# A two-layer convolution/attention hybrid on one core: the first image's tokens in the second image's bands, the last bands' linear layers between the attention's products

## The chip, the core and the metric

The kernel runs on one core of a Trainium2 chip. A core has a matrix engine (TensorE, here PE, with its weight loads PEld), a vector engine (VectorE, DVE), a scalar engine (ScalarE, ACT), a general engine (GpSimd, POOL) and a queue that issues DMA transfers (SyncE, SP; ACT issues some too). The engines run side by side, each works through its own instructions in order, and semaphores make one wait for another. Matrix products are written to PSUM, which has eight banks of 128 partitions by 512 floats.

The metric is device time in microseconds of one execution. Everything is computed in float32.

## What is computed

The input is two images of 128 channels on a grid of 64 by 64. Layer 0 works on positions of the grid, layer 1 on the same 4096 positions as a sequence of tokens. Cut to what matters (`_ln` is a layer norm over channels, `_na2d` an attention of four heads in which each position sees the 7 by 7 window around it):

```python
# layer 0
v = group_norm(x, G=32)                      # per image
r = v
y = _ln(v);  y = _na2d(y, qkv_w, qkv_b, rpb, proj_w, proj_b)
y = _ln(y);  y = y @ w1.T + bl1
v = y + r;   r = v
y = _ln(v);  y = relu(y @ w2.T + bl2)
y = _ln(y);  y = y @ w3.T + bl3
x = x + (y + r)
# layer 1, t = tokens of x
t = t + attention(_ln_t(t))                  # 4096 x 4096 with the diagonal masked,
t = t + spectral_ffn(_ln_t(t))               # long convolutions, four branches
```

The attention of layer 1 uses its normalised tokens as queries, keys and values alike. (In the reference's text the function for it is written for any length; here the length is 4096.)

## The kernel before

**Layer 0** goes through 16 bands: image 0 then image 1, eight bands of eight grid rows each. A band's work is cut into named pieces, and `PLAN` gives every piece a time. Band number k is shifted by k times `PERIOD`; all pieces of all bands are sorted by that time, and inside `tc.manual_schedule` the instructions of PE, DVE, ACT and POOL are issued in exactly this order. The numbers set only the order: nothing waits for a time. DMA issues on SP are not part of the manual order.

A band's pieces are

- `p.*`, the input: `p.xg` (group norm applied, POOL, line 445), `p.tok` (four transposes to tokens), layer norm (`p.bn` statistics, `p.pw` the power on POOL, `p.zd`/`p.za` the scaling on DVE and ACT, `p.tr` transposes back, `p.zT` copy), then `p.q`, `p.k`, `p.v` with their copies. `p.vc` also stores v to DRAM in eight transfers and loads the windows (`vw`, 98 positions each) in up to sixteen.
- `u0.*` to `u3.*`, the attention in four units of 128 positions: `S` the scores (line 515, sixteen small products in four banks), `t0` to `t3` adding the bias table with a minimum (DVE, line 528), `e0` to `e3` the exponentials (ACT, line 538), `T0`, `T1` turning them (PE, line 551), `c0`, `c1` copies (ACT and DVE), `V` the product with v (line 573).
- `r.*`, the division by the sums, ending in `r.att` (line 604), and `t.*`, the tail: projection, layer norm 1, `w1`, residual `t.x2`, layer norm 2, `w2`, relu, layer norm 3, `w3`, and `t.fin`, which writes the band back to `xa` (line 660). `t.add` on POOL adds the original x into `x2` (line 636).

The p-pieces of a band lie up to 2.4 periods ahead of its first unit, the tail ends 4.2 periods after it. The PSUM banks are dealt in rings: `ps_m` of five (`bank()`), `ps_t` of two (`tokens`), `ps_o` of one for the unit products.

**Between the layers** `tokens(0, bank)` makes layer 1's tokens of image 0: eight groups of four tiles, each with transposes of `xa` (line 190), an add on DVE that also brings in the constant row `b3row` (line 193), statistics (lines 151, 152, 161), scaling to `tok` (DVE, line 169), transposes (line 180) and a copy to `cm` (ACT, line 204). Its 32 steps are events after the last band's start, mixed with the last bands' tails.

**Layer 1** runs `attention(0, fill)`: blocks of products from `cm` (line 743), exponentials on ACT (line 750), turning (line 757), and products with `tok` (lines 771, 796). After every block `fill()` takes one step of waiting work: first what follows a finished chunk (`urgent`), then a list, `[filters(), tokens(1, bank)]`. Then the same for image 1, and last the convolution (line 1104 on).

At the start SP loads image 0 in four transfers, ACT the weights; 32 small transfers, 16 on each of the two, bring the relative position table into `rev`, which is cleared on POOL beforehand (line 131) and turned by PE (`flipped`, line 246). All of it uses the space of `tok` and `cm` of image 0.

Of the kernel before, what the change touches and what calls it, by code (L numbers as in the profile page):

```python
# [48 lines left out]
    "p.xg": -6335, "p.tok": -6075, "p.bn": -5991, "p.pw": -5688, "p.zd": -5538, "p.nb": -5465, "p.za": -5233,  # L49
    "p.tr": -5130, "p.zT": -4875, "p.k": -4750, "p.kT": -4353, "p.q": -4242, "p.qT": -4132, "p.v": -3805,  # L50
    "p.vc": -3550, "u0.S": 0, "u0.t2": 105, "u0.t0": 150, "u0.e2": 165, "u0.t1": 195, "u0.e0": 230, "u0.t3": 240,
    "u0.e1": 295, "u0.e3": 360, "u0.T0": 440, "u0.T1": 495, "u0.c0": 510, "u0.c1": 565, "u1.S": 662, "u0.V": 752,
    "u1.t1": 768, "u1.t2": 812, "u1.e1": 828, "u1.t0": 857, "u1.t3": 902, "u1.e0": 917, "u1.e2": 1021,
    "u1.e3": 1086, "u1.T0": 1178, "u1.T1": 1233, "u1.c0": 1248, "u1.c1": 1303, "u2.S": 1325, "u1.V": 1415,
    "u2.t3": 1430, "u2.e3": 1490, "u2.t2": 1494, "u2.t0": 1539, "u2.e2": 1555, "u2.t1": 1584, "u2.e0": 1620,
    "u2.e1": 1685, "u2.T0": 1765, "u2.T1": 1820, "u2.c0": 1872, "u2.c1": 1890, "u3.S": 1988, "u2.V": 2079,
    "u3.t0": 2092, "u3.t1": 2137, "u3.e0": 2152, "u3.t2": 2182, "u3.e1": 2235, "u3.t3": 2250, "u3.e3": 2310,
    "u3.e2": 2375, "r.rden": 2390, "r.rb": 2422, "u3.T1": 2455, "u3.T0": 2510, "u3.c1": 2525, "r.rdT": 2565,
    "u3.c0": 2580, "r.c": 2658, "u3.V": 2740, "r.att": 2935, "t.proj": 3483, "t1.bn": 3722, "t1.pw": 3862,
    "t1.nb": 4022, "t1.za": 4053, "t1.zd": 4279, "t1.tr": 4580, "t1.zT": 4726, "t.w1": 4848, "t.x2": 4958,  # L60
    "t.tx": 5048, "t.add": 5197, "t2.bn": 5244, "t2.pw": 5476, "t2.zd": 5668, "t2.nb": 5741, "t2.za": 5966,
    "t2.tr": 6925, "t2.zT": 7109, "t.w2": 7593, "t.y": 7759, "t.ty": 8175, "t3.bn": 8584, "t3.pw": 8837,
    "t3.zd": 9148, "t3.nb": 9220, "t3.za": 9256, "t3.tr": 9630, "t3.zT": 9880, "t.w3": 10880, "t.fin": 11057,
}
PERIOD = 2650
# [17 lines left out]
def kernel(  # L83
# [40 lines left out]
    b3row = fp.tile([P, P], F32, name="b3row")  # L124

# [5 lines left out]
    nc.gpsimd.memset(cm[0][0 : QT * QT, 0 : HEADS * NTAB * NTAB], 0.0)  # L131
# [49 lines left out]

    def tokens(b, bank):

        for n0 in range(0, NT, 4):
            pt = bank()
            for j in range(4):
                ph, f = divmod(n0 + j, FB)
                par, h = divmod(ph, 2)
                t0 = h * TH + 2 * f + par
                nc.tensor.transpose(  # L190
                    pt[:, j * P : (j + 1) * P], xa[b][:, t0 : t0 + 2 * FB * (P - 1) + 1 : 2 * FB], ident
                )
            nc.vector.tensor_tensor(
                tt[b][:, n0 : n0 + 4, :], pt.rearrange("p (j c) -> p j c", c=P),
                b3row.unsqueeze(1).to_broadcast([P, 4, P]), ALU.add,
            )
            yield
            stats = ln_statistics(tt[b][:, n0 : n0 + 4, :])
            yield
            ln_apply(tok[b][:, n0 : n0 + 4, :], tt[b][:, n0 : n0 + 4, :], stats)  # L200
            yield
            pt = bank()
            transposed(pt, tok[b][:, n0 : n0 + 4, :])
            nc.scalar.copy(cm[b][:, n0 * P : (n0 + 4) * P], pt)
            yield


    with ExitStack() as l0:
        wp = l0.enter_context(tc.tile_pool(name="l0_w", bufs=1))
        big = l0.enter_context(tc.tile_pool(name="l0_big", bufs=1))  # L210
        bp = l0.enter_context(tc.tile_pool(name="l0_band", bufs=2))
        ps_m = l0.enter_context(tc.tile_pool(name="l0_ps_m", bufs=5, space=PSUM))
        ps_t = l0.enter_context(tc.tile_pool(name="l0_ps_t", bufs=2, space=PSUM))
        ps_o = l0.enter_context(tc.tile_pool(name="l0_ps_o", bufs=1, space=PSUM))
        vdram = l0.enter_context(tc.tile_pool(name="l0_dram", bufs=1, space=bass.MemoryType.DRAM))
# [12 lines left out]
        tab = wp.tile([P, 6, HEADS, KEYS], F32, name="tab")  # L228
        for h in range(HEADS):
            for r in range(QT):  # L230
                lo, hi = 6 - min(r, 6), min(NTAB, 21 - r)
                src = bass.AP(
                    rpb_pad.tensor, (h * RPR + lo - 6 + r) * RPW + 50, [[1, QT], [RPW, hi - lo], [1, NTAB]]
                )
                (nc.sync if h % 2 else nc.scalar).dma_start(out=rev[r * QT : (r + 1) * QT, h, lo:hi, :], in_=src)
        nc.sync.dma_start(out=mask, in_=nc.inline_tensor(_window_masks(), "window_masks").ap())
        for c in range(4):
            nc.sync.dma_start(out=xa[1][:, c * 1024 : (c + 1) * 1024], in_=xin[1, :, c * 1024 : (c + 1) * 1024])

        def bank():  # L240
            return ps_m.tile([P, 512], F32, tag="bank", name="bank")

        def flipped(h):
            pb = bank()
            for half in range(2):
                nc.tensor.matmul(
                    pb[half * 64 : (half + 1) * 64, 0 : NTAB * NTAB], lhsT=flip[0:64, 64:128],
                    rhs=rev[:, h].rearrange("p n m -> p (n m)"), start=True, stop=True,
                )
            nc.scalar.copy(base[:, h].rearrange("p n m -> p (n m)"), pb[:, 0 : NTAB * NTAB])  # L250
# [28 lines left out]
        for i, (lo, be, col, row) in enumerate((  # L279
# [3 lines left out]
            pb = bank()  # L283
# [13 lines left out]
        pb = bank()  # L297
# [8 lines left out]
        wide = bp.tile([P, P], F32, tag="wide", name="wide", bufs=1)  # L306
        nc.vector.tensor_copy(wide, cb[:, C_3 : C_3 + 1].to_broadcast([P, P]))
        pb = bank()
        nc.tensor.transpose(pb[:, 0:P], wide, ident)
        nc.vector.tensor_copy(b3row, pb[:, 0:P])  # L310
# [3 lines left out]
        sp = l0.enter_context(tc.tile_pool(name="l0_s", bufs=2))  # L314
        mp = l0.enter_context(tc.tile_pool(name="l0_m", bufs=3))
        ls = l0.enter_context(tc.tile_pool(name="l0_ln", bufs=6))
# [21 lines left out]
        def to_tokens(src, ring=ps_t, tag="tokens"):  # L338
            pt = ring.tile([P, 512], F32, tag=tag, name="pt")
            for j in range(4):  # L340
                nc.tensor.transpose(pt[:, j * P : (j + 1) * P], src[:, j * P : (j + 1) * P], ident)
            return pt

        def linear(lo, zT):
            pl = bank()
# [3 lines left out]
        def group_norm(b):  # L349
# [11 lines left out]
            pb = bank()  # L361
# [6 lines left out]
            pb = bank()  # L368
# [15 lines left out]
        def norm_pieces(stage, src):  # L384
# [46 lines left out]
            def _(t, b, g):  # L431
                t[stage + "pz"] = bank()
# [25 lines left out]
        def _(t, b, g):  # L458
            t["qT"] = bp.tile([P, BAND], F32, tag="qT", name="qT", bufs=3)
# [12 lines left out]
        def _(t, b, g):  # L472
            pv = t["pv"] = bank()
# [7 lines left out]
        def _(t, b, g):  # L481
            v = bp.tile([P, 4, P], F32, tag="v", name="v")
# [11 lines left out]
        def windows(b, g):  # L494

            for u in range(4):
                vw = bp.tile([HK, 2, 2, P], F32, tag="vw", name="vw", bufs=6)
# [7 lines left out]
        def unit_pieces(u):  # L505
# [3 lines left out]
            def _(t, b, g):  # L509
                t[name + "S"] = [bank() for _ in range(HEADS)]  # L510
# [35 lines left out]
            def half_pieces(ch):  # L546
                @piece(f"{name}T{ch}")
                def _(t, b, g):
                    pt = t[f"{name}T{ch}"] = bank()
# [38 lines left out]
        def _(t, b, g):  # L588
            t["rb"] = bp.tile([P, 4 * HEADS, DH], F32, tag="rb", name="rb", bufs=1)
# [3 lines left out]
        def _(t, b, g):  # L593
            t["pr"] = to_tokens(t["rb"].rearrange("p a d -> p (a d)"), ps_m, "bank")

        @piece("r.c")
        def _(t, b, g):
            t["rdT"] = bp.tile([P, BAND], F32, tag="rdT", name="rdT", bufs=1)
# [8 lines left out]
        def _(t, b, g):  # L607
            pt = t["pp"] = ps_t.tile([P, 512], F32, tag="tokens", name="pt")
# [25 lines left out]
        def _(t, b, g):  # L634
            for nat, til in ordered(xa[b][:, rows_of(g)], t["x2"]):
# [25 lines left out]

        for _ in group_norm(0):
            pass
# [7 lines left out]
        for k, (b, g) in enumerate(order):  # L671
            t = {}
            for name, at in PLAN.items():
                events.append((at + k * PERIOD, lambda f=pieces[name], t=t, b=b, g=g: f(t, b, g)))
        for i in range(8):
            events.append((-1800 + 200 * i, lambda ci=4 + i // 4, h=i % 4: table(ci, h, nc.gpsimd)))
            events.append((2 * PERIOD + 600 * i, lambda ci=2 + i // 4, h=i % 4: table(ci, h, nc.gpsimd)))

        gn1, tok0 = group_norm(1), tokens(0, bank)
        for i in range(7):  # L680
            events.append((2 * PERIOD + i * PERIOD // 3 + 50, lambda: next(gn1)))
        for i in range(NT):
            events.append((len(order) * PERIOD + i * PERIOD // 11, lambda: next(tok0)))
        events.sort(key=lambda e: e[0])
        engines = mybir.EngineType
        with tc.manual_schedule(engines={engines.PE, engines.DVE, engines.Activation, engines.Pool}):
            for _, f in events:
# [12 lines left out]
    with ap_:  # L700
# [19 lines left out]
        tt[1] = tp.tile([P, NT, P], F32, name="tt1")  # L720
        tok[1] = tp.tile([P, NT, P], F32, name="tok1")
        cm[1] = tp.tile([P, T], F32, name="cm1")
# [314 lines left out]
        steps = [filters(), tokens(1, bank)]  # L1037
# [253 lines left out]
```

## Time and profile before

| | |
|---|---|
| time, median of 3 runs | 2351.79 us (2351.61 to 2353.13) |
| time of the profiled run | 2352.78 us |
| span in the profile | 2351.0 us |
| PE, PEld, DVE, ACT, POOL busy | 2248.0, 1371.9, 973.0, 791.5, 207.4 us |

By stage, in microseconds from the span's start:

| stage | from, to | PE busy | DVE busy | ACT busy | PE clock |
|---|---|---|---|---|---|
| loads, tables, group norm, first inputs | 0 to 57.3 | 32.35 | 23.34 | 12.03 | 0.91 |
| bands, first to last V product | 57.3 to 387 | 316.15 | 265.98 | 253.73 | 0.98 |
| last tails, tokens of image 0 | 387 to 450.5 | 34.95 | 41.57 | 14.01 | 0.72 |
| attention of layer 1, both images | 450.5 to 1416 | 942.63 | 377.41 | 257.05 | 0.99 |
| convolution and output | 1416 to 2351 | 921.93 | 264.75 | 254.65 | 0.99 |

In the profile a line is named L and its number. A float32 matmul is recorded as two instructions. "x8" behind a name counts merged instructions, "<-" stands before what released a wait, and an index behind a tile's name is left out. The clock is the share of full speed that PE was granted. Matmul ends are modelled, so PE counts as busy between products that follow each other closely.

### The profile page before, as it was taken

To read this page: it belongs to the slowest core of one execution; us is meant where nothing else is said; L and a number is where in the kernel's file an instruction comes from. 1 tells how busy PE (TensorE), PEld (TensorE's weight loads), DVE (VectorE), ACT (ScalarE), POOL (GpSimd) and SP (SyncE) were. 2 spreads that over 40 slices of the span, in tenths; PEclk is the share of its full clock that TensorE was granted. 3 is DMA by queue.
4 is the path that set the end of the run, shared out by engine and by line. 5 is a ranking of instruction groups with operands and counts; after the bars stand their busy time and mean duration, and the time that the engine had idled before them with its cause. 6 is when DMAs were issued, how large, how long until landed. Compare 5 with 4: busy or idle time off the path is not lost.

```text
span 2351.0 us, 32007 instructions
## 1 busy us (share of the span) xinstructions
PE 2248.0 (96%) x11977; PEld 1371.9 (58%) x11977; DVE 973.0 (41%) x3104; ACT 791.5 (34%) x1927; POOL 207.4 (9%) x286
## 2 busy tenths in 40 slices
PE   5899997699999999999999998999999999999998
PEld 3566665345544444454444444777777777777777
DVE  4688887524443334643333343222222323323233
ACT  2678875222222222322222222222223323223231
POOL 4344442200000000000000000000000000000000
PEclk9999998799999999999999999999999999999999
DMA  3111210220000001500000014222122122122101
GB/s 115 53 52 54 55 53 16 37 74 32 23 23 23 18 16 55 145 21 23 23 23 19 15 41 122 56 56 47 47 56 56 42 51 56 40 53 56 37 10 72
DMA packets 179565, 109.68 MB, mean 47 GB/s; under 512 B 30929, under 2 KB 164561, under 8 KB 178898
## 3 DMA queue, kind: packets, MB, share of 16 engines
q1 hardware_dynamic: 177104, 107.02, 17.2%
q8 instruction: 95, 1.56, 0.3%
q10 hardware_dynamic: 2306, 0.62, 0.1%
q14 instruction: 60, 0.49, 0.1%
HBM read 72.98 MB, written 34.60 MB: 46 GB/s over the span
## 4 chain that ended last, share of the span: by engine, by line
PE 87%; DVE 5%; POOL 2%; ACT 2%; issue 2%; DMA 1%; SPq 0%; POOLq 0%; ACTq 0%; DVEq 0%
PE acc L1115 24%; PE pc L1104 12%; PE bank L743 10%; PE own L771 9%; PE other L796 8%; PE bank L757 4%; PE bank L346 3%; PE bank L180 2%; PE py L1142 2%; PE bank L551 2%; PE bank L888 2%; PE bank L856 1%; ACT p L538 1%; PE bank L515 1%; PE bank L992 1%
## 5 line engine op out<-in xcount | busy, mean ns | idle before, releaser
L750 ACT ACTIVATE e<-bank 128x512 f32<-128x512 f32 x288 | 172.2, 598 | 602.7 <-PE bank L743 459.4
L1105 DVE COPY y<-pc 128x512 f32<-128x512 f32 x320 | 221.5, 692 | 358.8 <-PE pc L1104 355.1
L743 PE MATMUL bank<-cm 128*128 128x512 f32 x576 | 301.8, 609 | 0.9 <-DVE xa L660 0.9
L1104 PE MATMUL pc<-ct,ut 64*128 64x512 f32 x1280 | 287.2, 599 | 6.2 <-DMA ct<-gs 6.2
L1115 PE MATMUL acc<-y,mpl 128*128 128x256 f32 x1280 | 292.1, 382 | 0.0
L1115 PE MATMUL acc<-y,mmi 128*128 128x256 f32 x1280 | 288.0, 379 | 0.0
L1115 PEld LDWEIGHTS acc<-y,mpl 128*128 128x128 f32 x1280 | 238.1, 190 | 59.4 <-issue 29.6
L1115 PEld LDWEIGHTS acc<-y,mmi 128*128 128x128 f32 x1280 | 242.6, 190 | 32.6
L1105 ACT COPY y<-pc 128x512 f32<-128x512 f32 x320 | 205.2, 641 | 93.9 <-PE pc L1104 93.9
L796 PE MATMUL other<-e,tok 128*128 128x512 f32 x448 | 228.3, 592 | 0.0
L771 PE MATMUL own<-et,tok 128*128 128x512 f32 x448 | 227.1, 593 | 0.7 <-DVE part L760 0.7
L760 DVE CUSTOM_DVE_ANT_0 et<-bank,one 128x512 f32<-128x512 f32 x224 | 145.7, 688 | 182.4 <-PE bank L757 182.2
L1104 PEld LDWEIGHTS pc<-ct,ut 64*128 64x128 f32 x1280 | 121.8, 188 | 152.8 <-issue 147.6
L1121 ACT COPY ob<-acc 128x256 f32<-128x256 f32 x40 | 23.9, 597 | 430.8 <-PE acc L1115 430.8
L771 PEld LDWEIGHTS own<-et,tok 128*128 128x128 f32 x448 | 84.3, 190 | 108.5 <-issue 70.3
L796 PEld LDWEIGHTS other<-e,tok 128*128 128x128 f32 x448 | 85.1, 190 | 107.1 <-issue 107.1
L743 PEld LDWEIGHTS bank<-cm 128*128 128x128 f32 x576 | 97.8, 195 | 78.6 <-issue 49.5
L1154 DVE TENSOR_TENSOR xa<-py,xa 128x512 f32<-128x512 f32 x32 | 22.2, 692 | 281.4 <-PE py L1142 281.4
L757 PEld LDWEIGHTS bank<-ident,e 128*128 128x128 f32 x896 | 103.4, 141 | 56.4 <-issue 49.0
L538 ACT ACTIVATE p<-p,mn 128x196 f32<-128x196 f32 x256 | 114.9, 454 | 39.4 <-DVE mn L528 39.3
L757 PE MATMUL bank<-ident,e 128*128 128x128 f32 x896 | 116.9, 273 | 0.0
L152 POOL TENSOR_TENSOR ln_rs<-ln_rs,mhalf 128x4 f32<-128x4 f32 x32 | 32.4, 1011 | 956.6 <-DVE ln_rs L151 939.4
(181 smaller groups left out, 2375.4 us busy)
## 6 DMA issues: line engine op xcount, KB each, us to landing
ut<-us SPq DMA_DIRECT2D x80, 256.0 KB
us<-ub SPq DMA_DIRECT2D x64, 256.0 KB
vw<-vd SPq DMA_DIRECT2D x256, 49.0 KB
ct<-gs SPq DMA_DIRECT2D x160, 72.0 KB
ct<-gs SPq DMA_DIRECT2D x160, 64.0 KB
gs<-ub SPq DMA_DIRECT2D x20, 256.0 KB
xa<-in_x_dram SPq DMA_DIRECT2D x8, 512.0 KB
vd<-v SPq DMA_DIRECT2D x128, 32.0 KB
```

Of the source, the lines that this page charges most:

```text
L180: nc.tensor.transpose(ps[:, j * P : (j + 1) * P], src[:, j, :], ident)
L346: nc.tensor.matmul(pl, lhsT=wg[:, lo : lo + P], rhs=zT, start=True, stop=True)
L538: nc.scalar.activation(p, p, AF.Exp, bias=t[name + "mn"][:, h : h + 1], scale=-1.0, accum_out=t["den"][:, u, h : h + 1],)
L743: nc.tensor.matmul(ps, lhsT=cm[b][:, n * P : (n + 1) * P], rhs=cm[b][:, chunk(c)], start=True, stop=True)
L750: nc.scalar.activation(e, ps, AF.Exp, bias=0.0, scale=ASCALE, accum_out=part[:, n, c : c + 1])
L757: nc.tensor.transpose(pt[:, k * P : (k + 1) * P], es[k][:, m * P : (m + 1) * P], ident)
L760: nc.vector.tensor_tensor_reduce(et, pt, one, 1.0, 0.0, ALU.mult, ALU.add, part[:, n, a : a + 1])
L771: nc.tensor.matmul(own, lhsT=tok[b][:, n, :], rhs=e, start=first, stop=last)
L796: nc.tensor.matmul(other, lhsT=tok[b][:, 4 * CHUNKS[a] + j, :], rhs=es[j], start=(j == 0), stop=(j == 3))
L1104: nc.tensor.matmul(pc, lhsT=ut[fp, b, par, :], rhs=cv_[fp], start=True, stop=True)
L1105: (nc.scalar.copy if f else nc.vector.tensor_copy)(y[:, 4 * f : 4 * f + 4, :, par, b * 2 * FB + q : (b + 1) * 2 * FB : 2], pc.rearrange("p ...
L1115: nc.tensor.matmul(acc, lhsT=(mmi if l else mpl)[:, k, :], rhs=y[:, 1::2, k, ::-1, :] if l else y[:, 0::2, k, :, :], start=(l == 0 and k = ...
```

## The change

All of it is in layer 0 and in the passage to layer 1.

- **Tokens of image 0 in the bands of image 1.** New pieces `k.*`, only in bands 8 to 15: band 8 + g makes one group of four tiles. `halves` orders the groups so that the first four need only the upper half of image 0. Transposes (`k.a`), a copy on ACT (`k.tt`), statistics on DVE (`k.bn`), the power and the scaling on POOL (`k.pw`, `k.z`), transposes (`k.b`), a copy on ACT (`k.cm`). In `tokens`, still used for image 1, the add becomes a copy on ACT.
- **The constant row.** `b3row` goes; `t.add` first adds the constant to `x2`, on POOL.
- **The last tails.** The pieces due after band 15's `u3.V` are split: those of bands 13, 14 and 15 from `t.ty`, `t.tx` and `t.proj` on are put into `later`, 63 pieces; the rest (also all k-pieces) keep their place. `drain()`, the first in layer 1's list, issues three of them a step, taking banks from layer 1's ring, then frees layer 0's space and allocates `tt`, `tok`, `cm` of image 1.
- **New order.** Another `PLAN`, with `PERIOD` 2300. The p-pieces lie up to 1.9 periods ahead, the tail ends 5.2 periods after. Band 1's p-pieces are 2000 earlier, almost with band 0's.
- **First loads.** Clearing `rev`, its 32 loads, the masks and image 1 come later in the program, behind the constants.
- **Pools** are split so that the attention's tiles are freed at the end of the manual order and the tails' tiles at the end of `drain`.

```diff
 PLAN = {
-    "p.xg": -6335, ... "u0.S": 0, ... "u1.S": 662, "u0.V": 752, ... "u1.T0": 1178, ... "u2.S": 1325, ...
+    "p.xg": -4399, ... "u0.S": 0, ... "u1.S": 374, "u0.V": 586, ... "u2.S": 971, ... "u1.T0": 1207, ...
...
-PERIOD = 2650
+PERIOD = 2300
...
-            nc.vector.tensor_tensor(
-                tt[b][:, n0 : n0 + 4, :], pt.rearrange("p (j c) -> p j c", c=P),
-                b3row.unsqueeze(1).to_broadcast([P, 4, P]), ALU.add,
-            )
+            nc.scalar.copy(tt[b][:, n0 : n0 + 4, :].rearrange("p j c -> p (j c)"), pt)
...
         @piece("t.add")
         def _(t, b, g):
+            nc.gpsimd.tensor_scalar(t["x2"], t["x2"], cb[:, C_3 : C_3 + 1], None, ALU.add)
             for nat, til in ordered(xa[b][:, rows_of(g)], t["x2"]):
                 nc.gpsimd.tensor_tensor(til, til, nat, ALU.add)
...
+        @piece("k.a")
+        def _(t, b, g):
+            t["n0"] = halves[g]
+            t["ka"] = l0_bank()
+            token_tiles(0, t["n0"], t["ka"])
...
+        @piece("k.z")
+        def _(t, b, g):
+            for j in range(4):
+                nc.gpsimd.tensor_scalar(
+                    tok[0][:, t["n0"] + j, :], tt[0][:, t["n0"] + j, :], t["kmv"][:, j, 0:1], t["krs"][:, j : j + 1],
+                    ALU.subtract, ALU.mult,
+                )
...
+                if name[0] == "k" and b == 0:
+                    continue
+
+                early = PERIOD - 300 if k == 1 and name[0] == "p" else 0
+                events.append((at + k * PERIOD - early, k, name, lambda f=pieces[name], t=t, b=b, g=g: f(t, b, g)))
...
-        gn1, tok0 = group_norm(1), tokens(0, bank)
+        gn1 = group_norm(1)
...
-        for i in range(NT):
-            events.append((len(order) * PERIOD + i * PERIOD // 11, lambda: next(tok0)))
...
+        last = bands[-1] * PERIOD + PLAN["u3.V"]
...
+            (now if early else later).append(f)
...
-            for _, f in events:
+            for f in now:
                 f()
...
+        def drain():
+
+            rings[:] = [(ps_m, "bank")] * 2
+            for i, f in enumerate(later):
+                f()
+                if i % 3 == 2:
+                    yield
+            l0.close()
...
-        steps = [filters(), tokens(1, bank)]
+        steps = [drain(), filters(), tokens(1, bank)]
```

## The prediction

> **What bounds the kernel now.** First the page's slices.
>
> ```profile
> PE   5899997699999999999999998999999999999998
> PEclk9999998799999999999999999999999999999999
> ```
>
> TensorE (PE) is full except in the first slice and around slices 7 and 8 (58.8 us each), where its granted clock falls too. Next the busy time by stage; columns are length, then busy time of PE, PEld, DVE, ACT, POOL, then clock, DMA share, GB/s.
>
> ```profile
> 140.00:340.00 200.00, 198.64 (x2746) 136.74 (x2746) 170.40 (x840) 162.59 (x505) 89.66 (x124) 1.00 0.19 54
> 340.00:387.00 47.00, 44.36 (x643) 29.06 (x641) 34.76 (x169) 35.22 (x110) 13.57 (x22) 1.00 0.12 34
> 387.00:450.50 63.50, 34.95 (x124) 21.09 (x124) 41.57 (x180) 14.01 (x28) 17.26 (x23) 0.72 0.00 1
> ```
>
> The last attention product of layer 0 runs at 386.3, the first product of layer 1 (L743) at 450.5: 63.5 us at clock 0.72, PE busy 34.95. The waits of that stretch (total, times, longest) say why:
>
> ```profile
> POOL ln_rs L152 <- DVE ln_rs L151: 30.6, 7, 7.9
> ACT cm L204 <- PE bank L180: 25.2, 8, 8.3
> PE bank L180 <- DVE tok L169: 20.8, 7, 5.2
> ```
>
> The eight token groups of image 0 go one after another: transposes, statistics (DVE), power (POOL), scaling (DVE), transposes, copy (ACT). Each waits for the last; PE waits for DVE.
>
> The bands' pace is read from the end of each (L604, in three stretches):
>
> ```profile
> L604 DVE TENSOR_TENSOR att<-po,rdT x3: 685/690/692, 73.7 to 119.8; 128x512 f32<-128x512 f32 x3
> ...
> L604 DVE TENSOR_TENSOR att<-po,rdT x6: 686/690/693, 119.8 to 224.2; 128x512 f32<-128x512 f32 x6
> ...
> L604 DVE TENSOR_TENSOR att<-po,rdT x5: 689/690/691, 244.9 to 327.8; 128x512 f32<-128x512 f32 x5
> ...
> L604 DVE TENSOR_TENSOR att<-po,rdT x3: 686/690/691, 348.5 to 389.2; 128x512 f32<-128x512 f32 x3
> ```
>
> That is 23.05 us a band in the ramp, 20.9 and 20.7 in the middle, 20.35 at the end. "PE full" is partly modelled, though. The chain of waits shows pieces at speed:
>
> ```profile
> 376.49 0.81 ACT z L416 x2
> 377.30 1.78 ACT p L538 x8
> 379.12 0.97 PE bank L551 x7
> 380.53 0.91 PE bank L515 x16
> 381.43 0.58 PE po L573 x32
> 382.02 1.91 PE bank L346 x4
> ```
>
> Per band at such speeds: scores 4 x 0.75 (between 0.52 and 0.93), turning the probabilities 4 x 0.87, products with V 4 x 0.58, five linear layers x 0.86 (two passes of 0.43), V 0.95, projection 1.95, eight groups of four transposes x 0.44: 19.5 us, 18.6 with scores at 0.52. So 1.2 to 2.1 us of 20.7 is waiting: L551 waits for the eight exponentials that the chain shows ahead of it.
>
> **What the Trainium skill says.** "TensorE: Matmul & The Clock Gate", Part 1: the array runs at half clock by default, and again after an idle window of about 3.4 us. The trace agrees: clock 0.72 in the tail, and the first ten passes of L743 take 7.06 us there, against 4.3 at 0.43. "GPSIMD Engine Reference", 3.1: about 2.6 cycles an element for a two-input operation, so POOL is a poor place for elementwise work. The trace has 999 ns for 128x384 of that kind, 609 ns for a one-input copy of 128x512, and 1666 ns for the strided two-scalar 128x384 (L445). "DMA: Bandwidth & Descriptors", Latency: about 2 us fixed per transfer; here the first V windows cost 2.44 us (vw<-vd at 56.41) after their last issue.
>
> **The change, part by part** (its own span, 2351.0 us, against 2351.79 median: I add 0.8 at the end).
>
> *First loads and first two bands.* Before, x is in by about 15 us, the group norm ends at 20.8, two input stages follow, the first scores start at 47.8, the first V product at 57.35. Putting the bias-table loads (32 issues, 0.79 us each on ACT, 0.58 on SP) behind the weights frees the first loads: at best 1.5 us, the clearing of the table (1.4 us on POOL) now coming behind the other constants. On SP they pass behind the mask and half of image 1, and end at about 18 us; the flips need them only after both xg (POOL 2.44 each plus 1.3 for a power), near 29. Two bands together give PE unbroken work from 29, so it warms earlier: flips 5.9, then 2 x 0.44, 4 x 0.86, 2 x 0.95 at speed are 12 us, scores at about 42. But both bands' V stores now stand together on SP: 16 x 0.6, four window loads x 0.75, 2.44 to land: first V at 42 + 15 = 57, as before. Band 0 then ends after 14 to 15 us: 72 (before 73.7). Bands 1 to 3 are bounded by SP: 8 x 0.56 + 16 x 0.75 = 16.5 us each, below PE and ACT with few tails yet; I take 18.5 (16.5 to 23).
>
> *New order.* Two units' scores now stand ahead of the first one's turning, so the eight exponentials overlap other products. PE's wait falls but DVE (170.4/200 x 20.75 = 17.7 us a band) and ACT (16.9) are close. I take 19.6 (18.6 to 20.75).
>
> *Tokens in the second image.* Per band PE gains 8 transposes = 0.88 us, DVE 1.25 (four statistics 0.89, aggregates 0.36, as L392 and L394 in the chain), ACT two copies x 0.59, POOL a power 1.27 and four scalings: not in the trace in this form; 0.3 to 0.8 each (a quarter of copy, or L445's 798 for 128x128); 0.8 taken, 3.2. `t.add`'s new 128x512 scalar add: 0.6 (copy) to 2.2 (1666 x 512/384); 2 taken. POOL goes from 9.3 to 15.8 of 20, hidden beside PE. Queued behind k.z on POOL are the next band's xg and powers, which have over half a period of slack. DVE reaches 18.9, ACT 18.1. I take 20.4 for the bands with everything (19.5 to 21.6).
>
> *Tails.* By the plan 63 pieces of the last three bands come after the attention's start, in 21 steps. On PE: one projection 1.9, six linear layers 5.2, eleven transpose groups 4.8: 11.9 us, none hidden, since PE is full there; DVE and ACT work is (41% and 33% busy over the run). The tokens of image 1 end at 693 in an attention that runs half as long again, so 22 more of its steps fit. Stalls in it: 0 to 33 (22 x 1.5); 5 taken.
>
> *b3row* goes (wide, transpose, two copies: 0.5 us, in the first waits): nothing.
>
> *Sum.* Band 0 at 72; +3 x 18.5 = 127.5; +5 x 19.6 = 225.5; +5 x 20.4 = 327.5; +2 x 19.6 = 366.7; V ends 2.3 earlier (as 386.9 to 389.2): 364.4. Then what is left in the old stage: 6.1 us of PE, in a chain t3 statistics 1.2, powers and k.z queued on POOL (0.6 + 2 + 1.3 + 1.3 + 3.2, from the last reciprocal on), k.b, two linear layers: 15 us (12 to 18; layer 1's first small loads stand in DVE's order there). Attention at 379.4: 71.1 earlier. Minus 11.9, minus 5, plus 4 of the 6.6 us lost before to the cold start (2.8) and the filter's load (idle 465.3 to 468.3, then 0.8):
>
> ```profile
> 457.58 1.02 PE L771 MATMUL own<-e,tok 128*128 128x512 f32 x2
> ...
> 468.34 1.12 PE L992 MATMUL bank<-ph,fr 128*128 128x512 f32 x2 [2.88 <-DVE ph L985]
> ```
>
> 58.2 gained: 2351.0 - 58.2 + 0.8 = 2293.6; I say 2293.
>
> **Rivals.** *The bands don't speed up* (DVE and ACT at 90% bind with the queues as they are). For it: the same engines, more work; against: the wait for exponentials is visible. Last end 389.2 + 8 x 0.88 = 396.2, attention 408.9, 41.6 earlier, minus 12.9: 2323.
> *Drained pieces stall the attention:* each step's transposes wait on a chain of statistics, power and scaling of some 4.5 us in in-order queues; against: steps stand 3.2 us apart and the other products fill. 33 in place of 5: 2321.
> *Everything at its floor:* 70, 3 x 17.4, 5 x 18.7, 5 x 19.5, 2 x 18.7 = 350.6, 13 us of rest: attention 361.3, 89.2 - 11.9 + 6.6 gained: 2268.
> *Slower: the ring of five PSUM banks.* The scores of two units, both turnings, and now k.a and k.b draw on it; each take waits for DVE or ACT to empty the fifth before. The trace has such waits of 0.8 to 1.5 us (L515 behind L551 and L558). Four of 0.8 a band cost 48 us on top of the first rival: 2371. It decides from 1.9 us a band over the old pace (28.7 / 15), that is 22.7. Against: the score banks are emptied first, by short L528s (0.36).
> *The change doesn't move the tokens:* the instruction order shows them in the bands; none left ahead of the attention but the last group.
>
> **How the numbers follow.** Main 0.58, bands as before 0.20, stalls 0.09, floor 0.06, ring 0.07. Main's own range is 2275 to 2312 (0.7 us in 14 bands is 10, ramp 6, rest 5); with the first three rivals 2266 to 2325. 0.2% is 4.7 us, what this measurement tells from no change: faster 0.92, same 0.01, slower 0.07.
>
> **What would show it.** Last L604 near 367; middle steps 19.6 and 20.4; about 15 us to the first attention product; clock near 1 there; 12 us of L346, L180, L341 after it. Wrong if steps stay 20.7, if POOL or a bank stands ahead of PE in the bands, or if PE idles between the drained pieces.

## The result, and the profile after

| | before | after |
|---|---|---|
| time, median | 2351.79 us | 2372.61 us (2371.73 to 2379.95) |
| span in the profile | 2351.0 us | 2371.0 us |
| start of `att` in the first and the last band | 73.7, 389.2 us | 79.5, 450.1 us |
| first attention product (L743, L822) | 450.5 us | 463.6 us |
| from there to the end | 1900.5 us | 1907.4 us |

The change makes the kernel slower: ratio 1.0094, 95% interval 1.0074 to 1.0115. 2293 was forecast. The loss is in the bands. The page's slices of the kernel after (58.8 us each before, 59.3 here; the slices that count are the first eight):

```profile
PE   4788888899999999999999998999999999999998
PEclk9799999999999999999999998999999999999999
```

Before, TensorE was at 9 from the third to the sixth slice, and the dip stood at slices 7 and 8, ahead of the attention. Now that dip is gone, but all the band slices are at 8. By stage (length, then busy time of PE, PEld, DVE, ACT, POOL, then clock, DMA share, GB/s):

```profile
140.00:340.00 200.00, 171.92 (x2268) 116.96 (x2267) 142.16 (x704) 134.15 (x414) 97.99 (x126) 0.91 0.16 44
340.00:447.20 107.20, 93.24 (x1328) 64.57 (x1327) 82.44 (x415) 77.25 (x242) 63.02 (x85) 0.97 0.14 38
447.20:463.50 16.30, 10.26 (x32) 4.78 (x32) 9.60 (x43) 5.37 (x13) 13.58 (x17) 0.79 0.35 101
```

In the middle bands PE is busy for 171.92 of 200 us, where it was 198.64, and its clock is 0.91, where it was 1.00. The stage between the layers has shrunk from 63.5 us to 16.3, as meant. The pace of the bands, from the end of each (the line has moved from L604 to L605):

```profile
L605 DVE TENSOR_TENSOR att<-po,rdT x4: 680/681/682, 79.5 to 160.2; 128x512 f32<-128x512 f32 x4
L605 DVE TENSOR_TENSOR att<-po,rdT x5: 682/682/682, 180.1 to 278.3; 128x512 f32<-128x512 f32 x5
L605 DVE TENSOR_TENSOR att<-po,rdT x5: 680/682/682, 304.6 to 406.8; 128x512 f32<-128x512 f32 x5
L605 DVE TENSOR_TENSOR att<-po,rdT x2: 680/686/692, 431.2 to 450.1; 128x512 f32<-128x512 f32 x2
```

(450.1 - 79.5) / 15 = 24.7 us a band, where 20.7 was usual. What PE waits for is one thing. The waits of the bands, 57 to 447 us (total, times, longest), hold two lines that the kernel before did not have:

```profile
PE po L574 <- DMA vw<-vd: 50.3, 27, 7.7
PEld po L574 <- DMA vw<-vd: 47.6, 28, 3.1
```

The products with V wait for their windows of v to come back from DRAM: 97.9 us of PE and its weight load added, against 2.7 in the kernel before. Most of these are the same waits, seen on both; PE alone stands for 50.3 us, 7.7 of them in the first band. The timeline shows one of these waits. First SP, the queue that issues the stores of v (L486) and the loads of the windows (L503); columns are start, length, instructions merged:

```profile
231.72 13.61 SPq L503 DMA_DIRECT2D vw<-vd  x8
246.79 4.96 SPq L486 DMA_DIRECT2D vd<-v  x8
251.85 10.32 SPq L503 DMA_DIRECT2D vw<-vd  x13
```

Then PE over the same time (the bracket is the idle time before it, and what ended it):

```profile
244.65 1.06 PE L476 MATMUL bank<-w_sb,zT 128*128 128x128 f32 x8
245.54 0.60 PE L179 MATMUL bank<-ident,z 128*128 128x128 f32 x4
...
253.87 0.85 PE L574 MATMUL po<-pT,vw 98*32 98x64 f32 x24
257.69 0.32 PE L574 MATMUL po<-pT,vw 98*32 98x64 f32 x8 [2.98 <-DMA vw<-vd]
257.94 1.11 PE L179 MATMUL bank<-ident,z 128*128 128x128 f32 x4
```

And the chain of waits there (start, length, what):

```profile
251.85 0.79 SPq L503
252.74 0.78 SPq L503
253.57 0.72 SPq L503
254.35 0.72 SPq L503
255.12 2.53 DMA vw<-vd
258.01 1.05 PE bank L179 x4
```

`p.v` (L476) of a band is done at 245.5 on PE. Its copy on ACT lets the stores start at 246.79; eight stores take 4.96, four loads 3.3, the last one lands 2.53 later: 12.2 us from the end of `p.v`. The consumer is `u0.V` of the band before, because a band's windows reach into the next band's rows. In the new order PE has only some 9 us of other work between the two, so it waits 2.98, and the pieces after the wait run at half speed (1.11 in place of 0.60 for four transposes). The next band's `p.v` then comes some 13 us of PE work after that `u0.V`: 12 and 13 make the 25 us of a band. SP is not too slow here (it stands idle from 245.33 to 246.79, until v is there), nor in the other bands: from the fourth on it is free before ACT has copied v in all but one, and there it comes 0.1 us late. The path through it is too long for the place that `p.v` now has.

The passage to layer 1 is as meant: the first ten passes of the attention take 4.53 us (7.22 before), and the drained pieces (here L610 and L612) lie between the products without a gap:

```profile
463.57 4.53 PE L822 MATMUL bank<-cm 128*128 128x512 f32 x10 [0.94 <-DVE xa L662]
467.94 1.02 PE L850 MATMUL own<-e,tok 128*128 128x512 f32 x2
468.80 1.02 PE L610 MATMUL bank<-prow,e 128*128 128x512 f32 x2
469.65 1.05 PE L612 MATMUL bank<-w_sb,att 128*128 128x128 f32 x8
470.55 1.02 PE L822 MATMUL bank<-cm 128*128 128x512 f32 x2
```

### The profile page after: what moved, and what is told of

Its sections match the earlier page's. It is cut to its first block, busy times and chain, and to the rows that moved or that the text cites. A ratio compares the mean times of both kernels' runs of the same rounds, so it can differ in the third digit from the quotient of the medians.

```text
span 2371.0 us, 31914 instructions
## 1 busy us (share of the span) xinstructions
PE 2238.8 (94%) x11976; PEld 1368.1 (58%) x11976; DVE 953.4 (40%) x3046; ACT 796.6 (34%) x1943; POOL 259.3 (11%) x342
## 4 chain that ended last, share of the span: by engine, by line
PE 82%; SPq 5%; DVE 4%; ACT 2%; DMA 2%; POOL 2%; issue 2%; POOLq 0%; DVEq 0%; ACTq 0%
PE acc L1208 24%; PE pc L1197 12%; PE own L850 9%; PE bank L822 9%; PE other L875 8%; PE bank L836 4%; SPq L486 3%; PE bank L179 2%; PE bank L347 2%; PE py L1235 2%; SPq L503 2%; PE bank L967 2%; PE bank L935 1%; DMA vw<-vd 1%; PE bank L552 1%
## 5 line engine op out<-in xcount | busy, mean ns | idle before, releaser
L822 PE MATMUL bank<-cm 128*128 128x512 f32 x576 | 296.3, 598 | 0.9 <-DVE xa L662 0.9
L850 PEld LDWEIGHTS own<-et,tok 128*128 128x128 f32 x448 | 84.2, 190 | 110.2 <-issue 69.5
L822 PEld LDWEIGHTS bank<-cm 128*128 128x128 f32 x576 | 95.6, 192 | 73.0 <-issue 44.1
L151 POOL TENSOR_TENSOR ln_rs<-ln_rs,mhalf 128x4 f32<-128x4 f32 x24 | 24.3, 1011 | 879.6 <-DVE ln_rs L150 879.6
L539 ACT ACTIVATE p<-p,mn 128x196 f32<-128x196 f32 x256 | 114.5, 451 | 16.5 <-DVE mn L529 16.5
```

The lines of the kernel that those rows point to most:

```text
L539: nc.scalar.activation(p, p, AF.Exp, bias=t[name + "mn"][:, h : h + 1], scale=-1.0, accum_out=t["den"][:, u, h : h + 1],)
L822: nc.tensor.matmul(ps, lhsT=cm[b][:, n * P : (n + 1) * P], rhs=cm[b][:, chunk(c)], start=True, stop=True)
L850: nc.tensor.matmul(own, lhsT=tok[b][:, n, :], rhs=e, start=first, stop=last)
```

## The experiments

The theory (A in the expectations): the new order puts `p.v` and `p.vc` too near to the first product that needs their windows, and the serial path copy, stores, loads, landing sets the pace. Against it stand the order as such, the extra work on POOL, and the tails. All runs were made beside the kernel before (medians 2350.8 to 2351.8).

| run | what it is | median, us | ratio to before, 95% |
|---|---|---|---|
| after | the change | 2372.6 | 1.0074 to 1.0115 |
| e1_v_early | after, `p.v` and `p.vc` early | 2325.8 | 0.9872 to 0.9901 |
| e12_v_half | half of that distance | 2336.2 | 0.9922 to 0.9952 |
| e2_before_v_late | before, `p.v` and `p.vc` late | 2430.0 | 1.0310 to 1.0344 |
| e7_act_stores | after, every second store of v on ACT | 2349.6 | 0.9989 to 1.0007 |
| e3_after_no_drain | after, no tails in the attention | 2392.4 | 1.0158 to 1.0189 |
| e4b_old_order | after, in the old order | 2330.4 | 0.9894 to 0.9924 |
| e8_old_order_old_loads | and the first loads as before | 2328.3 | 0.9890 to 0.9920 |
| e5_old_order_no_add | e4b without the POOL add | 2317.3 | 0.9841 to 0.9871 |
| e6_v_early_no_add | e1 without the POOL add | 2322.6 | 0.9865 to 0.9898 |
| e10_old_order_row | e8 with the constant row on DVE | 2315.8 | 0.9836 to 0.9869 |
| e11_old_order_row_no_drain | and no tails in the attention | 2328.8 | 0.9893 to 0.9922 |
| e9_v_early_row_old_loads | e1 with old loads and the row | 2329.3 | 0.9894 to 0.9923 |

### V early in the new order

```diff
-    "p.v": -2705, "p.vc": -2643,
+    "p.v": -3470, "p.vc": -3420,
```

> The changed kernel with only p.v and p.vc moved up, to right behind p.k: v's stores and window loads then start 777 plan units (a third of a band) earlier. Theory A (the V windows arrive late, one serial loop per band from p.v over stores and loads to u0.V): waits of L574 for vw fall from 97.9 us to under 20, the step between ends of bands from 24.7 to 19 to 20.5 us, time 2285 to 2310. Theory B (DVE and ACT at 90% or PE's order itself bind, the V product is only where it shows): step stays 24 to 25, time 2360 to 2375, the waits move to L516 and L552.

2325.8 us: 46.8 gained by two numbers, and the kernel is faster than before. The waits of L574 in the two kernels, first after, then e1 (us, times):

```profile
  DMA vw<-vd: 97.9, 55
```

```profile
  DMA vw<-vd: 9.0, 10
```

So the lost lead is what made the change slower than the kernel before. But the time is 16 us above what was expected at most: a band now takes 21.5 us, not 19 to 20.5. Over 160 to 260 us (length, busy time of PE, PEld, DVE, ACT, POOL, clock, DMA share, GB/s):

```profile
160.00:260.00 100.00, 91.58 (x1368) 62.62 (x1369) 84.09 (x410) 78.40 (x240) 51.88 (x67) 1.00 0.20 53
```

PE is free for 8.4 of 100 us. Its largest wait there is for exponentials:

```profile
PE bank L552 <- ACT p L539: 5.5, 5, 1.1
```

### V late in the old order

An edit of the kernel before, with nothing of the change in it.

```diff
-    "p.v": -3805, "p.vc": -3550,
+    "p.v": -3120, "p.vc": -2960,
```

> The kernel before with only p.v and p.vc moved later, so that the distance from p.vc to the u0.V that needs its windows is 1062 plan units in place of 1652 (8.3 us of the old pace in place of 12.9; the changed kernel has 929 of 2300, 8 us at 20 us a band). Theory A: stores 5.0, four loads 3.0, landing 2.4 and copy 0.8 need 11.2 us, so V waits 1.5 to 3 us a band; L573 waits for vw 15 to 45 us, time 2365 to 2395. Theory B: the old order has slack elsewhere, time 2350 to 2355.

2430.0 us, 78 slower than the kernel before and 35 above the range. The waits for windows are back (80.7 us in 43 waits, 37.5 of them on PE; 15 to 45 were expected), a band takes about 26 us, and the attention starts at 528.8. The same cause works in the other order. Its size was underrated. The waits of PE are half of the loss; the mean clock, 0.973 where the kernel before has 0.982, fits a second cost, half speed after a wait (see the last section), but no run prices that part alone.

### Half the distance

```diff
-    "p.v": -2705, "p.vc": -2643,
+    "p.v": -3100, "p.vc": -3040,
```

> The changed kernel with p.v and p.vc moved half as far as in the first experiment (-3100 and -3040, which adds some 3.7 us of work on PE to the 8.4 between a band's v and the band before's first product with windows). Theory A, a serial path of stores, window loads and landing of 11.5 to 12 us against what PE has in between: nearly all the waits vanish, 2325 to 2340, waits of the V products for windows below 25 us. Rival, a gain in proportion to the distance: about 2349, waits about 50 us.

2336.2 us, waits for windows 19.7 in 11: half the distance brings 36.4 of the 46.8 us and nearly nine tenths of the waits' fall. So it is a bound to be passed and not a slope. The five kernels in one table. The lead is the distance in the plan from `p.vc` to `u0.V` of the band before, as a share of the period, times 20 us for a band's work on PE, an estimate (after: 586 - 2300 + 2643 = 929 of 2300, 8.1 us):

| | lead, us | waits for windows, us (PE and weight load added) |
|---|---|---|
| after | 8.1 | 97.9 |
| e2_before_v_late | 8.0 | 80.7 |
| e12_v_half | 11.5 | 19.7 |
| before | 12.5 | 2.7 |
| e1_v_early | 14.8 | 9.0 |

The waits go where the lead reaches the 12 us that the path takes. (What is left in e1 lies mostly in the first bands.)

### Stores on two queues

```diff
-                nc.sync.dma_start(
+                (nc.scalar if i % 2 else nc.sync).dma_start(
                     out=vd[b][g * QT : (g + 1) * QT, c * QT : (c + 1) * QT, :],
```

> The changed kernel with every second store of v issued from ACT right behind the copy, in place of SP (four of eight a band, 0.57 us each); p.v stays where it is. Theory A (one serial loop: copy, stores, loads, landing, u0.V): the loop is 2 to 2.5 us shorter, step 24.7 to 22.2 to 23, time 2335 to 2350, waits of V for vw 98 to 55 to 70. Theory B (engines at their limit): ACT gets 2.3 us more a band, time 2372 or more.

2349.6 us, 23 better than after. This shortens the path on SP and leaves the order as it is. The waits of the products for windows fall to 3.8 us, further than expected, but now ACT stands still, and PE behind it (waits over 57 to 430):

```profile
ACT zT L439 <- DMA vd<-v: 27.3, 10, 2.9
...
PE bank L516 <- ACT zT L439: 13.5, 10, 1.5
...
ACT pT L559 <- DMA vd<-v: 11.0, 4, 2.8
```

The name of a DMA in these lines misleads: ACT doesn't wait for a store to land. The timeline of ACT shows what fills the time:

```profile
227.96 0.56 ACT L484 COPY v<-bank 128x512 f32<-128x512 f32 x1
228.55 2.60 ACTq L486 DMA_DIRECT2D vd<-v  x4
231.19 0.59 ACT L439 COPY zT<-bank 128x512 f32<-128x512 f32 x1 [2.67 <-DMA vd<-v]
```

Of the 2.67 us between the two copies, ACT spends 2.60 on issuing its four stores, some 0.6 us each, and it goes on as soon as the fourth is out; so it is in all 16 bands. ACT works through its queue in order, the issues included. So the cost that theory B names is there (2.3 us a band expected), beside theory A's gain: the path was shortened, at the cost of an engine on the way of everything.

### The old order

```diff
-    "p.xg": -4399, "p.tok": -4382, "p.bn": -4336, "p.pw": -4194, "p.zd": -3861, "p.nb": -3836, "p.za": -3811,
...
+    "p.xg": -6335, "p.tok": -6075, "p.bn": -5991, "p.pw": -5688, "p.zd": -5538, "p.nb": -5465, "p.za": -5233,
...
-PERIOD = 2300
+PERIOD = 2650
...
-                early = PERIOD - 300 if k == 1 and name[0] == "p" else 0
+                early = 0
```

All pieces have their numbers of before; those of `k.*` are the new ones times 2650 / 2300.

> The changed kernel with the old order: the PLAN numbers and PERIOD of before for p, u, r and t, the k-pieces at their own places scaled by 2650/2300, band 1's input not advanced. Tokens in the bands, deferred tails and first loads stay as changed. Theory A: V windows in time as before, step 20.5 to 20.9 in the first image and up to 21.7 in the second, first attention product at 400 to 412, time 2305 to 2325. Theory B (k-pieces and the added POOL work overload the bands): step in the second image 23 or more, time 2335 or more.

2330.4 us, above the range by 5, and the attention starts at 419.2, where 412 was the latest expected. The tokens, the tails, the POOL add and the loads are in, and V waits for windows for 3.8 us only: the new order with V where it was put costs 42.2 us. The bands of image 0 take 21.4 here and 20.7 before, those of image 1 22.6. What holds them is on POOL. A stretch in image 1 (start, length; `rb`, the new add, the residual, then the power of another band's layer norm):

```profile
316.04 0.61 POOL L688 COPY rb<-rden 128x512 f32<-128x512 f32 x1 [2.14 <-PE bank L439]
316.63 1.57 POOL L733 TENSOR_SCALAR x<-x,cb 128x512 f32<-128x512 f32 x1
318.28 1.42 POOL L735 TENSOR_TENSOR x<-x,xa 128x128 f32<-128x128 f32 x2
319.68 0.22 POOL L497 TENSOR_SCALAR ln_rs<-ln_mv 128x4 f32<-128x4 f32 x1
319.98 1.04 POOL L498 TENSOR_TENSOR ln_rs<-ln_rs,mhalf 128x4 f32<-128x4 f32 x1
```

The statistics for that power were ready on DVE at 318.3. The power comes at 319.7, and DVE's scaling waits until 321.05 with the rest of DVE behind it. Over the kernel that scaling waits for POOL (us, times):

```profile
  POOL ln_rs L498: 24.9, 21
```

In four bands of image 0 (140 to 225 us) it is 3.8 us in 4 waits, where the kernel before has 0.3 in 1.

### Without the POOL add

```diff
-            nc.gpsimd.tensor_scalar(t["x2"], t["x2"], cb[:, C_3 : C_3 + 1], None, ALU.add)
```

This kernel leaves out the adding of layer 0's last constant (that of `w3`).

> e4b_old_order with one operation left out: the new scalar add of t.add on POOL (128x512, 1.57 us a band; so the constant of w3 is not added). In e4b the bands of the first image, which have no k-pieces, took 21.4 us and not 20.7 as before. Theory C (the longer POOL queue delays the powers, and DVE's scaling waits for them: 16 us in e4b): step back to 20.7 in the first image, 0.5 to 0.7 less in the second, time 2316 to 2324. Theory D (POOL is hidden, as the prediction had it): 2328 to 2333.

2317.3 us: 13.1 gained, and the same wait is less than half:

```profile
  POOL ln_rs L498: 9.4, 9
```

16 adds of 1.57 us are 25 us of POOL, which was busy for 11% of the kernel and for half of the bands (52.31 of 100 us in e4b); half of these 25 us shows in the time. The bands of image 0 are back at 20.7. Two of them in e4b, and below them two in this run (length, busy time of PE, PEld, DVE, ACT, POOL, clock, DMA share, GB/s):

```profile
164.90:207.50 42.60, 42.35 (x571) 28.89 (x570) 35.20 (x177) 33.82 (x105) 22.19 (x29) 1.00 0.21 59
160.30:201.70 41.40, 41.15 (x570) 28.28 (x569) 35.35 (x177) 33.57 (x105) 18.99 (x27) 1.00 0.21 59
```

PE does the same work in both and counts as busy but for 0.25 us in both, yet one takes 1.2 us longer. The whole difference lies in the scores: each product taken to the start of the next, they hold PE for 7.0 us in e4b and for 5.8 here. So a wait can lie inside time that counts as busy.

In the new order the same edit (again the constant is left out) was expected to be worth less, since other waits lead there:

> e1_v_early with the same scalar add left out. Its chain of waits names no POOL instruction in the bands, so both theories C and D expect little here: 2321 to 2328. If it falls below 2318, POOL sets the new order's pace too.

2322.6 us, 3.2 gained on e1.

### The first loads

In e4b, `rev`'s clearing, its 32 loads, the masks and image 1 go back ahead of the constants.

> e4b_old_order with the first loads in the old place (the clearing of rev first, the 32 table loads, masks and image 1 ahead of the constants). The first band of e4b ended at 75.6, of the kernel before at 73.7. If the moved loads cost that: 1 to 3 us faster than e4b, 2326 to 2330. If they gain, as the prediction allowed (at best 1.5 us): 2331 to 2333.

2328.3 us, 2.1 less than e4b, which is less than the intervals of the two leave open (some 3.5 us each way). In the two traces the first `att` starts at 70.4 in place of 75.6 and the attention 5 us earlier. But that start differs from run to run by 2.6 us: e10 and e11 below, alike up to there and with the loads in the old place too, have 71.3 and 73.9, and e5, with the moved loads, has 73.5. So no gain of the moved loads shows, and no cost clear of the spread.

### Tails

```diff
-            (now if early else later).append(f)
+            now.append(f)
```

> The changed kernel with all tails issued before the attention (nothing is put into later). If the deferred tails are worth what the prediction says (they save a serial tail of some 20 us with little PE work and cost 11.9 us inside the attention): first L822 12 to 25 us later, attention shorter by 7 to 12, time 2376 to 2390. If the deferred pieces stall the attention by more than they save: 2355 to 2371.

2392.4 us, 2.4 above the range that goes with a useful drain. Without the drain the attention starts at 498.9, 35.3 later, and takes 1894.5 from there, 12.9 less: the 63 pieces cost 12.9 us in the attention and 35.3 ahead of it, more than the 25 expected at most. Median against median the drain is worth 19.8.

### The row on DVE, and the tokens alone

```diff
-            nc.gpsimd.tensor_scalar(t["x2"], t["x2"], cb[:, C_3 : C_3 + 1], None, ALU.add)
...
-            nc.scalar.copy(tt[0][:, t["n0"] : t["n0"] + 4, :].rearrange("p j c -> p (j c)"), t["ka"])
+            nc.vector.tensor_tensor(
+                tt[0][:, t["n0"] : t["n0"] + 4, :], t["ka"].rearrange("p (j c) -> p j c", c=P),
+                b3row.unsqueeze(1).to_broadcast([P, 4, P]), ALU.add,
+            )
```

This is made on e8; `b3row` is built as in the kernel before, and `tokens` adds it for image 1. The second kernel also has the edit of e3.

> The changed kernel with three parts undone: the old order and period (k pieces scaled to it), the first loads in their old place, and the constant brought in as before by the row added on DVE in k.tt, with no scalar add on POOL. What remains of the change is the tokens in the bands and the last tails in the attention. Theory C (the POOL add costs about 13 us in the old order, the moved loads 2, the row's add on DVE next to nothing): 2328.3 - 13 = 2313 to 2320. If instead the row's add on DVE (eight adds of about 0.6 us, where ACT copied) hurts as the POOL add did: 2325 or more.

> The kernel before it in this list, with all tails kept ahead of the attention: what remains of the change is the tokens in the bands alone. Theory D (deferring the tails is worth some 20 us, as 2392.4 against 2372.6 showed in the new order): 2334 to 2342, so moving the tokens alone gains 10 to 18. Rival: the tokens in the bands bring nothing, since the tails fill the stage that they leave: 2350 or more.

2315.8 us for the first (ratio 0.9852, 0.9836 to 0.9869), the lowest median of all runs here. What remains is the kernel before with the tokens in the bands and the tails in the attention. Its bands are as full as those of before, over the same 100 us as e1's above:

```profile
160.00:260.00 100.00, 98.81 (x1362) 68.36 (x1361) 86.40 (x431) 80.00 (x248) 48.51 (x66) 1.00 0.20 54
```

2328.8 us for the second: the tokens alone gain 22, more than was expected, and the tails another 13.0, less than in the new order. A band with a token group takes 21.4 to 21.5 us, one without 20.7. The attention takes 1892.7 us here and 1906.5 with the drain: 13.8 for the pieces.

### The new order without these costs

e1 with the first loads in their old place and the row on DVE.

> The changed kernel with p.v and p.vc early as in the first experiment, the first loads in their old place and the constant as a row on DVE: the new order with the three costs found taken away. Theory A: 2325.8 - 3 (no POOL add) - 2 (loads) = 2317 to 2322, level with the old order, so the new order brings no gain of its own. Rival, as the prediction had it (new order worth 1.1 us in each of 15 bands against the old): 2300 to 2308.

2329.3 us, above both ranges, and 13.5 us slower than the old order with the same parts (e10). Its first `att` starts at 77.6 (71.3 in e10), the next three steps are 21.7, 21.7 and 28.5 (21.9, 23.4 and 21.4), the later ones 21.2 and 21.9 (20.7 and 21.4). Taking off the POOL add and the moved loads and putting the row in brings nothing on e1 (2325.8): costs measured in one order don't carry over to another. The row's add on DVE goes with faster bands of image 1 in the old order (21.4 in e10; 21.8 in e5, whose copy is on ACT) and with slower ones in the new (21.9; 21.3 in e6), all four without the POOL add. Why isn't shown.

What the new order is worth, with V early, depends on the other parts too:

| parts | new order | old order |
|---|---|---|
| POOL add, moved loads | 2325.8 (e1) | 2330.4 (e4b) |
| no add, moved loads | 2322.6 (e6) | 2317.3 (e5) |
| row on DVE, old loads | 2329.3 (e9) | 2315.8 (e10) |

The new order loses less to the POOL add (3.2 us against 13.1), and with it is 4.6 us the faster one (the four times of e1 all lie below the four of e4b). Against the best kernel of the old order it brings no gain.

## Why the prediction was wrong

**The sum.** By starts of `att` and of the attention, predicted and measured, with what V's early place (e1) leaves of it:

| term | predicted | after | miss | miss in e1 |
|---|---|---|---|---|
| band 0 ends | 72 | 79.5 | 7.5 | 6.6 |
| bands 1 to 3 | 3 x 18.5 = 55.5 | 80.7 | 25.2 | 16.7 |
| bands 4 to 8 | 5 x 19.6 = 98 | 118.1 | 20.1 | 9.2 |
| bands 9 to 13 | 5 x 20.4 = 102 | 128.5 | 26.5 | 6.0 |
| bands 14, 15 | 2 x 19.6 = 39.2 | 43.3 | 4.1 | -0.9 |
| last `att` to the attention | 12.7 | 13.5 | 0.8 | 0.8 |
| attention to the end | 1913.4 | 1907.4 | -6.0 | -5.7 |

(The predicted last two rows follow from its 379.4 for the attention's start and 58.2 gained.) 84.2 us were lost ahead of the attention, 6 won after it, 78 in all. In e1 it is 33 in all, so some 46 of the 78 is V's lead.

**"New order ... I take 19.6".** This is the step that failed, twice over. First, it counted PE, DVE and ACT, and never followed `p.vc` to its consumer. The prediction had all the prices: 0.6 a store, 0.75 a load, 2.44 to land. It added them up for the first two bands; for bands 1 to 3 it took only SP's sum, 16.5 us a band, and for the middle bands, which are longer than that, nothing of SP. But a queue that has time to spare can still be a path that is too long: 8 stores, 4 loads and a landing are 10.8 us after ACT's copy, and they have to fit between two named pieces of the order. The Trainium skill ("DMA: Bandwidth & Descriptors", section "Rules for kernel authors") says to issue the DMA early, compute, and wait late; the new order does the reverse for this one, and the five leads above show its price.

Second, "1.2 to 2.1 us of 20.7 is waiting", and the new order was to win it. In the timeline of before, PE's pieces of two bands (200 to 241.4), each taken to the start of the next, sum to 41.4 us with no idle time marked: 20.7 a band. As e4b and e5 show, that can still hold waits. The same count gives 39.7 in e1, with 3.3 idle of 43.0: the new order runs the scores faster (4.3 us in two bands, 5.9 before), and all its pieces together take 0.85 us a band less. That is what it wins; but it pays 1.65 a band for marked waits, for exponentials (L552) for the most part. "Two units' scores now stand ahead of the first one's turning" holds for one pair alone: in the new plan those of `u1` and `u2`. `u0` and `u3` are turned with no other scores in between, and at `u3` PE waits in each of these two bands of e1 (the first one, from its scores to its turning):

```profile
226.28 0.59 PE L516 MATMUL bank<-kT,qT 32*64 32x196 f32 x16
...
229.94 1.08 PE L552 MATMUL bank<-ident,p 128*98 128x128 f32 x8 [1.09 <-ACT p L539]
```

So the wait that the order was thought to remove is one that it has. ("The eight exponentials" are four, one for each head, and four instructions that read out their sums.) The sum of pieces at speed, 18.6 to 19.5, was low as well: by the count above eight groups of transposes take 4.0 a band, taken as 3.5, the turning 4.0, taken as 3.5, and the five linear layers 4.6, taken as 4.3.

**The first bands.** 18.5 was taken for bands 1 to 3, "bounded by SP". In e1, free of most waits for windows, they take 22.0, 21.7 and 28.4. In the long one PE waits 1.85 us for exponentials and 1.10 and 1.31 for POOL's group norm of the next input (`xg`), which follows the power of image 1's own group norm in POOL's queue. Its clock is 0.57 from 137 to 141 us and 0.50 from 144 to 150. Over that stretch the trace shows no other cause, but no run tests it. First scores came at 45.9 (42 predicted), the first V product at 58.4 (57), and the band ended 21 us after it, where 14 to 15 was taken. The loads, "at best 1.5 us" of gain, brought none that shows (e8).

**Work on POOL.** 2 us for the new add was a little high (1.57), 0.8 for `k.z` right (0.80). "Hidden beside PE" was wrong for the add: it costs 13 us in the old order (e5), since powers stand behind it on POOL, and DVE and PE behind these. `k.z` wasn't taken out alone.

**Tokens in the bands.** 0.8 us a band was the difference taken (20.4 against 19.6); the old order shows 0.7 to 0.8. The stage ahead of the attention fell to 13.5 us after the last `att`, 12.7 predicted. This part held, and gains 22 us by itself. It was right for the reason given: the eight groups no longer go one after another with PE idle.

**Tails and the attention.** 11.9 of PE and 5 of stalls were taken, 16.9 in all; 12.9 and 13.8 were measured: PE's work is not hidden, and beside 11.9 of it 1 to 2 us are left for stalls, an estimate. The gain from a warm start and the filter's load was taken as 4; against the kernel before, the attention without drained pieces takes 6.0 less (e3) to 7.8 less (e11).

**The rivals.** The ring of five banks gave 2371, next to the 2372.6 measured, by the wrong mechanism: in e1 weight loads of scores still wait for ACT to empty a bank (25.0 us in 34 waits, 18.9 in 26 in after), and the time is 47 us less. A number that is met proves no cause. No rival held the loop through SP. The bound of the range on the slower side lacked it for that reason.

## What to carry to other kernels

When a piece is moved in an order, follow all that it issues to whoever waits for it: price that path end to end, and set it against the work that the new order leaves in between, in the steady loop and not only at the start. A queue's load says nothing on this. Before a new order is credited with the removal of a wait, find for each place where the engine waits what the new order puts in between there, and don't take a full row of the profile for a proof that nothing waits. And work on an engine that is busy for a tenth of the kernel, or half of a band, isn't hidden if short operations that everyone needs stand behind it.

## What the runs showed of the hardware

A wait of 2.98 us costs more than itself. Windows of two microseconds around the one shown above (after; columns as before, the clock stands before the last two):

```profile
254.00:256.00 2.00, 0.61 (x24) 0.29 (x20) 2.00 (x11) 0.00 (x0) 1.67 (x3) 1.00 0.18 53
256.00:258.00 2.00, 0.31 (x9) 0.22 (x10) 0.34 (x4) 0.00 (x0) 0.00 (x0) 0.97 0.25 72
258.00:260.00 2.00, 2.00 (x7) 1.41 (x7) 0.00 (x0) 0.91 (x3) 0.00 (x0) 0.50 0.21 61
260.00:262.00 2.00, 2.00 (x22) 0.92 (x20) 0.75 (x1) 1.70 (x8) 0.00 (x0) 0.67 0.22 65
```

The clock is 1.00 through the wait, 0.50 after it, and back at 1.00 from 262 on: 2 x 0.5 and 2 x 0.33 make 1.7 us of lost work, which is half speed for about 3.3 us. The Trainium skill ("TensorE: Matmul & The Clock Gate", Part 1) gives about 3.4 us for an idle window and for the warm-up. The length of this slow phase agrees; the waits ahead of slow phases are shorter than that. In e1 one of 1.85 us was followed by a clock of 0.56, and in the kernel before one of 1.47 us (for exponentials, up to 96.5) by 0.51 from 97.5 to 101.0. Other slow phases are twice as long: in after, with a wait for windows from 208.6 to 211.2, the clock is 0.51 from 210.1 to 217.0. In a loop with such a wait in each band the slow phases come to some 1.3 to 1.7 us a band, an estimate: 1.7 by the windows above, and PE was idle 3.5 us of the 24.7 (28.1 of 200), its pieces take 19.9 at speed (as in e1), and 1.3 are left.
